# Two graph layers on one core: nodes kept features first, in two halves, between the layers

## The chip, the cores and the metric

The kernel runs on one core of a Trainium2 chip. The core has a matrix engine (TensorE, PE in the profile; its weight loads are PEld), a vector engine (VectorE, DVE), a scalar engine (ScalarE, ACT), GpSimd (POOL) and a sync engine (SyncE, SP) that issues most of the DMA. They run side by side, each in the order of its own instructions, and wait for one another by semaphores. The metric is the device time in microseconds (us); lower is better. One execution was also taken by the hardware profiler; its page and its trace are read here.

## The reference

There are 6250 nodes with 64 features each, and 206250 edges with 16 attributes for the first layer and 64 for the second. Cut to what matters:

```python
h = relu(layernorm(x))
# layer 0: messages along edges, summed at their targets, then a small MLP with batch norm
ea  = edge_attr_16 @ W_edge.T + b_edge
agg = segment_sum(relu(h[src] + ea), dst)
u   = (h + agg) @ W1.T + b1
u   = relu(gamma * (u - mean(u, 0)) * rsqrt(var(u, 0) + 1e-5) + beta)
x   = x + u @ W2.T + b2
h   = relu(layernorm(x))
# layer 1
Y = relu(concat(h[src], edge_attr_64) @ M_W.T + M_b)
Z = segment_sum(Y, dst)
x = x + relu(concat(h, Z) @ U_W.T + U_b)
```

The layer norms have no weights and go over a node's 64 features. The batch norm goes over all nodes, so nothing behind it can start before the whole of layer 0's sums are there.

## The kernel before, in words

The nodes lie in 49 blocks of 128 (NP is 6272), the edges in 101 groups of 16 x 128.

**Sort and layer 0.** Groups 0 to 70 are sorted: POOL scatters their rows by indirect DMA (L786) into a table ordered by block, and 35 blocks are read back, seven chunks each. Such a chunk (class Sorted) turns source and target into one-hot matrices (hot_s L413, hot_d L432) and lets TensorE fetch the sources from the table in SBUF, `tab`, which holds each row as three bf16 parts, and sum the messages (msg L443, L444). Groups 71 to 100 are not sorted (class Direct): POOL gathers their source rows from the table in DRAM (L518, 16 gathers a group, 476 in a layer), and DVE makes the one-hot matrix of the targets (hot_g L565); in layer 0 the message is msg_d (L578), in layer 1 it is made in the gathered tile itself (L574, L575). Work tiles hot_d and msg have two buffers, hot_g and msg_d two more. The gathered tiles have four buffers in layer 0 and five in layer 1. `pace` (L149) ties gathers to TensorE's progress. The end of a block in layer 0 is linear_0 (L809): a product with w1, the bias on ACT into the lower 64 partitions of acc (L816), and batch norm statistics of the block (L820).

**Order.** The sort and layer 0 are written under a manual schedule: PE, DVE and ACT keep the written order there. Everything behind it, the stage between the layers and layer 1, is put in order by a list scheduler (`in_order` L130, L1052), engine by engine, when the kernel is built. SP's loads and stores come in the order of the scheduler too.

**The general case.** `general` (L593) is a loop for edges that found no place. Its count, any_i (L956), is 0 or 49 and is read at run time; here it is 0, so that the loop is entered and left.

**Between the layers (L950 to L1023).** The maximum of the marks gives any_i. The statistics are put together (L980 to L991) to a scale and a shift for each of 64 features, held in 64 partitions. ACT applies them with the relu in place, seven pieces of 64 x 896 (L994). Then a loop over seven chunks of eight blocks: eight products py with a block of acc as the weights (64 x 128) and w2 as the 64 columns moved, so that nodes come to the partitions (L1007); x is loaded (L1009), b2 and py are added (L1010, L1011), and the new x is stored as x1 (L1012); `norm_relu` (L242) makes the layer norm over the free axis; `transposed` (L263) turns the result back to features first in h1t, by eight transposes and two copies on ACT; eight products pt (L1018) make the rows of layer 1's table, mb is added (L1020), the rows are stored to table1 (L1022) and split into the three bf16 parts of tab (L274). The gathers of layer 1 need all of table1.

**Layer 1.** Sorted chunks and Direct halves again, then for each block the output (L1026): two products with uh and uz, the bias, relu and x1 added, a store to out. After it the second call of `general`.

Of the kernel before, what the change touches and what calls it, by code (L numbers as in the profile page):

```python
# [45 lines left out]
P = 128  # L46
D = 64
N = 6250
E = 206250
NB = 49  # L50
NP = P * NB
GT = 16
NG = 101
# [43 lines left out]
def gnn_kernel(  # L97
    ctx: ExitStack,
    tc: tile.TileContext,
    x: bass.AP,  # L100
    src: bass.AP,
    dst: bass.AP,
# [10 lines left out]
    b2: bass.AP,  # L113
    mw_t: bass.AP,
    mb: bass.AP,
    uw_t: bass.AP,
# [154 lines left out]

    tab = const.tile([P, NB, 3, D], BF16, name="tab")

# [267 lines left out]
    class Direct:  # L541
# [20 lines left out]
        def targets(self):  # L562
            n = self.n
            self.hot = self.pool.tile([P, 8, P], F32, name="hot_g", bufs=2)
            nc.vector.tensor_tensor(self.hot[:, :n, :], slot_p[:, None, :].to_broadcast([P, n, P]),  # L565
                                    rel_d[:, self.k:self.k + n, None].to_broadcast([P, n, P]),
                                    op=OP.is_equal)

        def messages(self):
            n = self.n  # L570
            half = slice(8 * self.h, 8 * self.h + n)
            if self.layer == 1:
                self.msg = self.gat[:, half, :]
                nc.vector.tensor_add(self.msg, self.msg, self.ea[:, half, :])  # L574
                nc.scalar.activation(self.msg, self.msg, AF.Relu)  # L575
                return
            self.msg = msg = self.pool.tile([P, 8, D], F32, name="msg_d", bufs=2)[:, :n, :]
            nc.vector.tensor_add(msg, self.pm[:, :n, :], self.gat[:, half, :])  # L578
            nc.scalar.activation(msg, msg, AF.Relu)
            e1 = self.pool.tile([P, 8, D], F32, name="e1", bufs=2)  # L580
            nc.scalar.copy(e1[:, :n, :], self.pe[:, :n, :])
            load(terms[self.g, :, 8 * self.h * D:(8 * self.h + n) * D],
                 e1[:, :n, :].rearrange("p t d -> p (t d)"))
# [6 lines left out]
    marked = const.tile([P, NT], BF16, name="marked")  # L590
    any_i = const.tile([1, 1], I32, name="any_i")

    def general(layer, table, done):  # L593
        blocks = nc.values_load(  # L594
            any_i[0:1, 0:1], min_val=0, max_val=NB,
            skip_runtime_bounds_check_because="it is 0 or NB")
        with tc.tile_pool(name=f"rest{layer}", bufs=1) as rest:
            at_f = rest.tile([P, 1], F32, name="at_f")
            nc.vector.memset(at_f, 0.0)
            delta = rest.tile([P, P], F32, name="delta")  # L600
            with tc.For_i(0, blocks, 1) as b:
                nc.vector.memset(delta, 0.0)
                with tc.For_i(0, NG, 1) as g:
# [39 lines left out]
                    nc.vector.tensor_add(delta, delta, pa[:, 0, :])  # L643
                done(b, delta, rest)
                nc.vector.tensor_scalar(at_f, at_f, float(P), None, op0=OP.add)
# [4 lines left out]
    acc = const.tile([P, NP], F32, name="acc")  # L650
    stats = const.tile([D, NB, 6], F32, name="stats")

    with tc.tile_pool(name="sort", bufs=1) as sort:
# [155 lines left out]
        def linear_0(d):  # L809

            to = acc[:, d * P:(d + 1) * P]

            def product():
                p = bank([D, P], "u_p", "tr")
                mm(p, w1_sb, to, start=True, stop=True)
                nc.scalar.activation(to[:D, :], p, AF.Identity, bias=b1_c)  # L816

            def statistics():
                if d < NB - 1:
                    nc.vector.bn_stats(stats[:, d, :], to[:D, :])  # L820

            return [product, statistics]
# [32 lines left out]
        w1_sb = stacked(w1_t, "w1_sb")  # L855
        b1_c = column(b1, "b1_c")
        for j0, j1 in chunks:
# [43 lines left out]
    for g in range(GS, NG):  # L901
# [5 lines left out]
                                   op0=OP.is_lt, op1=OP.mult)  # L907

    def unsorted(layer, table, steps, per_half, behind, window_of, done):

# [37 lines left out]


    most = ln.tile([P, 1], F32, name="most")  # L950
    nc.vector.tensor_reduce(most, marked, AX.X, OP.max)
    p = bank([P, P], "most_p", "tr")
    nc.tensor.transpose(p, most.to_broadcast([P, P]), ident)
    any_f = ln.tile([1, 1], F32, name="any_f")
    nc.vector.tensor_reduce(any_f, p[0:1, :], AX.X, OP.max)
    nc.vector.tensor_scalar(any_i, any_f, float(NB), None, op0=OP.mult)  # L956

    w2_sb = weight(w2_t, "w2_sb")
    mx_sb = weight(mw_t[0:D, :], "mx_sb")
    uh_sb = weight(uw_t[0:D, :], "uh_sb")  # L960
    uz_sb = stacked(uw_t[D:2 * D, :], "uz_sb")
    b2_b = spread(b2, "b2_b")
    mb_b = spread(mb, "mb_b")
    ub_b = spread(ub, "ub_b")
    gamma_c = column(gamma, "gamma_c")
    beta_c = column(beta, "beta_c")

    def more_0(b, delta, pool):
        p = bank([D, P], "u_p", "tr")
        mm(p, w1_sb, delta, start=True, stop=True)  # L970
        u = pool.tile([D, P], F32, name="u")
        nc.vector.tensor_copy(u, acc[:D, ds(b * P, P)])
        nc.vector.tensor_add(u, u, p)
        nc.vector.tensor_copy(acc[:D, ds(b * P, P)], u)
        s = pool.tile([D, 1, 6], F32, name="s")
        nc.vector.bn_stats(s[:, 0, :], u)
        nc.vector.tensor_copy(stats[:, ds(b, 1), :], s)

    general(0, table0[:, :], more_0)
    nc.vector.bn_stats(stats[:, NB - 1, :], acc[:D, (NB - 1) * P:N])  # L980


    mv = ln.tile([D, 2], F32, name="mv")
    nc.vector.bn_aggr(mv, stats.rearrange("d s k -> d (s k)"))
    bn_scale = ln.tile([D, 1], F32, name="bn_scale")
    bn_shift = ln.tile([D, 1], F32, name="bn_shift")
    nc.scalar.activation(bn_scale, mv[:, 1:2], AF.Sqrt, bias=eps[:D])
    nc.vector.reciprocal(bn_scale, bn_scale)
    nc.vector.tensor_mul(bn_scale, bn_scale, gamma_c)
    nc.vector.tensor_mul(bn_shift, mv[:, 0:1], bn_scale)  # L990
    nc.vector.tensor_sub(bn_shift, beta_c, bn_shift)  # L991
    for a in range(0, NP, NP // 7):
        b = a + NP // 7
        nc.scalar.activation(acc[:D, a:b], acc[:D, a:b], AF.Relu, bias=bn_shift, scale=bn_scale)  # L994


    table1 = dram.tile([NP, D], F32, name="table1")
    table1_rows = table1.rearrange("(j p) d -> p j d", p=P)
    late = ctx.enter_context(tc.tile_pool(name="late", bufs=1))
    h1t = late.tile([D, NP], F32, name="h1t")  # L1000
    x1 = dram.tile([NP, D], F32, name="x1")
    x1_rows = x1.rearrange("(j p) d -> p j d", p=P)
    for j0, j1 in chunks:
        n = j1 - j0
        py = bank([P, 8, D], "py", "gp", 2)
        for j in range(j0, j1):
            mm(py[:, j - j0, :], by_node(acc)[:D, j, :], w2_sb, start=True, stop=True)  # L1007
        xs = ln.tile([P, 8, D], F32, name="xc", bufs=2)[:, :n, :]
        nc.sync.dma_start(xs, x_rows[:, j0:j1, :])  # L1009
        nc.vector.tensor_add(xs, xs, b2_b[:, None, :].to_broadcast([P, n, D]))  # L1010
        nc.vector.tensor_add(xs, xs, py[:, :n, :])  # L1011
        nc.sync.dma_start(x1_rows[:, j0:j1, :], xs)  # L1012
        h = ln.tile([P, 8, D], F32, name="h", bufs=2)
        norm_relu(h, xs)
        transposed(h1t, h, j0, j1)
        pt = bank([P, 8, D], "pt", "gp", 2)
        for j in range(j0, j1):
            mm(pt[:, j - j0, :], by_node(h1t)[:, j, :], mx_sb, start=True, stop=True)  # L1018
        tabf = ln.tile([P, 8, D], F32, name="tabf", bufs=2)
        nc.vector.tensor_add(tabf[:, :n, :], pt[:, :n, :],  # L1020
                             mb_b[:, None, :].to_broadcast([P, n, D]))
        nc.sync.dma_start(table1_rows[:, j0:j1, :], tabf[:, :n, :])  # L1022
        split(tabf, j0, j1)  # L1023


    def output(h_t, z_t, x_b, to, pool):  # L1026
        po = bank([P, D], "po", "pm", 2)
        mm(po, h_t, uh_sb, start=True, stop=False)
        mm(po, z_t, uz_sb, start=False, stop=True)
# [6 lines left out]

    def update(d):
        def product():
            z = acc[:, d * P:(d + 1) * P]
            x_b = late.tile([P, D], F32, name="x_b", bufs=2)  # L1040
            load(x_b, x1_rows[:, d, :])
            output(h1t[:, d * P:(d + 1) * P], z, x_b, out[d * P:(d + 1) * P, :], late)

# [11 lines left out]

    def more_1(b, delta, pool):
        z = pool.tile([P, P], F32, name="z")
        h_t = pool.tile([D, P], F32, name="h_t")
        x_b = pool.tile([P, D], F32, name="x_b")
        nc.vector.tensor_copy(z, acc[:, ds(b * P, P)])  # L1060
        nc.vector.tensor_add(z, z, delta)
        nc.vector.tensor_copy(h_t, h1t[:, ds(b * P, P)])
        nc.sync.dma_start(x_b, x1[ds(b * P, P), :])
        output(h_t, z, x_b, out[ds(b * P, P), :], pool)

# [62 lines left out]
```

## Time and profile before

| what | value |
|---|---|
| nine runs, median | 3138.66 us (3131.61 to 3139.53) |
| profiled execution, own time | 3132.79 us |
| its span | 3131.0 us |
| mean granted tensor clock | 0.819 |
| busy: PE, DVE, ACT, POOL | 2016.7, 1680.4, 641.2, 2066.0 us |
| scatters of the sort on POOL | 37.28 to 1618 us |
| gathers of layer 0 on POOL | 1621.7 to 2216.4 us |
| last statistics of layer 0 | 2222.3 us |
| first gather of layer 1 | 2330.98 us |
| last store to out issued | 3120.17 us |

The page gives each engine's busy time and, for 40 equal slices of the span, its busy tenths. A row of a group of instructions reads: line, engine, operation, what it writes and reads with shapes, how often; then busy time and mean duration of one in ns; then how long the engine had stood idle just before them and what ended that. A row of waits reads: engine, what it wanted to write and its line, who released it, the total in us, how often, the longest. Idle time of an engine that bounds nothing costs nothing, so each stage is read by itself.

### The profile page before, as it was taken

The page shows a single profiled execution, that of the slowest core. Times are in us where ns is not written, and L with a number is a line of the kernel's source. Part 1 is how long each engine was busy: PE and PEld are TensorE (multiplying, and loading weights), DVE is VectorE, ACT ScalarE, POOL GpSimd, SP SyncE. Part 2 cuts the span into 40 slices and gives each one's busy share as a digit, 9 for nine tenths or more (in the row PEclk, how much of TensorE's full clock was granted, in tenths as well). Part 3 has the DMA queues.
Part 4 walks back from the last instruction along what each step waited for, and adds up shares of the span by engine and source line. Part 5 has one row for each costly group of instructions (what it writes and reads, how often), then busy time and mean ns, then how long its engine had stood idle before and what let it go on. Part 6 is the DMA issues. An engine that isn't in the chain of part 4 may idle for free. (4 is left out here: it accounts for less than half of the span.)

```text
span 3131.0 us, 55390 instructions
## 1 busy us (share of the span) xinstructions
PE 2016.7 (64%) x20553; PEld 1589.8 (51%) x20553; DVE 1680.4 (54%) x3532; ACT 641.2 (20%) x1373; POOL 2066.0 (66%) x2098
## 2 busy tenths in 40 slices
PE   2457665575775757576769655555564767776677
PEld 2345554464554545365547444344454656665566
DVE  5756564564765647465625222212343757776576
ACT  2212221121221212122212111111221222222221
POOL 4777777777777777777777777777217456666471
PEclk8688887797887878798889877777657888888798
DMA  9788776888788877788657333333225666776573
GB/s 215 189 233 236 229 205 188 217 238 252 212 229 219 245 197 225 193 239 234 206 175 255 107 84 84 85 87 87 59 59 171 222 199 212 235 232 209 177 249 116
DMA packets 323511, 587.50 MB, mean 188 GB/s; under 512 B 101796, under 2 KB 175908, under 8 KB 314276
## 3 DMA queue, kind: packets, MB, share of 16 engines
q1 hardware_dynamic: 247956, 502.83, 53.3%
q0 software_dynamic: 66816, 79.02, 11.4%
q10 hardware_dynamic: 8464, 2.05, 0.5%
q8 instruction: 163, 2.67, 0.4%
q14 instruction: 112, 0.92, 0.1%
HBM read 382.71 MB, written 200.98 MB: 186 GB/s over the span
## 5 line engine op out<-in xcount | busy, mean ns | idle before, releaser
L786 POOL DMA_INDIRECT place<-to,ix x1136 | 1153.2, 1015 | 458.8 <-issue 241.2
L518 POOL DMA_INDIRECT gat<-table,src_d x952 | 904.7, 950 | 442.1 <-issue 376.4
L141 PE MATMUL pa<-hot_d,msg 128*64 128x128 f32 (+1 forms) x5250 | 716.8, 332 | 116.3 <-ACT msg L444 88.0
L141 PEld LDWEIGHTS pa<-hot_d,msg 128*64 128x64 f32 (+1 forms) x5250 | 551.2, 168 | 179.6 <-ACT msg L444 105.5
L432 DVE TENSOR_TENSOR hot_d<-cbank,dl 128x1024 f32<-128x1024 f32 (+1 forms) x490 | 537.4, 1102 | 124.0 <-PE pa L141 122.4
L141 PEld LDWEIGHTS <-hot_s 128*128 128x128 bf16 x5250 | 202.8, 104 | 304.0 <-DVE hot_s L413 196.2
L141 PE MATMUL gp<-tab,hot_s 128*128 128x64 bf16 x5250 | 217.3, 202 | 150.3 <-DVE hot_s L413 150.3
L141 PE MATMUL gp<-tab,st 128*128 128x64 bf16 x5250 | 224.7, 200 | 52.2 <-DVE msg L443 43.7
L578 DVE TENSOR_TENSOR msg_d<-pm_d,gat 128x512 f32<-128x512 f32 (+1 forms) x60 | 41.2, 687 | 403.6 <-DMA gat<-table,src_d 381.9
L141 PE MATMUL gp<-we,at 128*128 128x512 f32 (+1 forms) x490 | 257.2, 609 | 0.0
L141 PEld LDWEIGHTS <-st 128*128 128x128 bf16 x5250 | 193.3, 103 | 97.9 <-issue 84.3
L141 PE MATMUL pm_d<-we,ea_d 128*128 128x512 f32 x120 | 101.0, 937 | 203.9 <-DVE msg_d L578 203.9
L413 DVE TENSOR_SCALAR hot_s<-st,pcol 128x1024 bf16<-128x1024 bf16 (+1 forms) x245 | 122.5, 500 | 201.8 <-DMA hots<-hot_s 173.3
L444 ACT ACTIVATE msg<-msg 128x512 f32<-128x512 f32 (+1 forms) x245 | 141.8, 584 | 356.8 <-DVE msg L443 346.7
L141 PEld LDWEIGHTS pm<-we,ea 128*128 128x128 f32 x1136 | 179.8, 229 | 28.0 <-DMA ea<-in_ea 17.4
L141 PE MATMUL rk<-half,below 128*128 128x98 bf16 x142 | 19.3, 223 | 270.2 <-DVE half L712 270.2
L141 PE MATMUL pm<-we,ea 128*128 128x128 f32 x1136 | 180.0, 313 | 18.2 <-DMA ea<-in_ea 18.2
L294 ACT COPY at<-at_p 128x128 f32<-128x128 f32 (+1 forms) x245 | 64.6, 264 | 569.5 <-PE at_p L293 564.2
L443 DVE TENSOR_TENSOR msg<-gp,eb 128x512 f32<-128x512 f32 (+1 forms) x245 | 151.5, 627 | 27.8 <-PE gp L141 17.8
L141 PEld LDWEIGHTS <-below 128*128 128x128 bf16 x142 | 14.3, 101 | 284.4 <-issue 263.6
L565 DVE TENSOR_TENSOR hot_g<-cbank,rel_d 128x1024 f32<-128x1024 f32 x120 | 144.7, 1206 | 4.0 <-PE pd L141 3.9
L574 DVE TENSOR_TENSOR gat<-gat,e 128x512 f32<-128x512 f32 (+1 forms) x60 | 40.7, 684 | 184.4 <-DMA gat<-table,src_d 142.1
(139 smaller groups left out, 2357.5 us busy)
## 6 DMA issues: line engine op xcount, KB each, us to landing
eb<-place SPq DMA_DIRECT2D x70, 2050.0 KB
place<-minus SPq DMA_DIRECT2D x35, 2050.0 KB
st<-src_rows SPq DMA_DIRECT2D x210, 256.0 KB
hots<-hot_s SPq DMA_DIRECT2D x210, 256.0 KB
st<-hots SPq DMA_DIRECT2D x210, 256.0 KB
ea<-in_ea SPq DMA_DIRECT2D x71, 512.0 KB
place<-to,ix POOLq DMA_INDIRECT x1136
ea_d<-in_ea SPq DMA_DIRECT2D x30, 512.0 KB
```

What stands on the lines that cost most here:

```text
L141: i = nc.tensor.matmul(*args, **kwargs)
L294: nc.scalar.copy(at[:n * ED, :], p[:n * ED, :])
L413: nc.vector.tensor_scalar(hot_s[:, :n, :], st[:, :n, :], pcol, None, op0=OP.is_equal)
L432: nc.vector.tensor_tensor(self.hot_d[:, :n, :], slot_p[:, None, :].to_broadcast([P, n, P]), self.dl[:, self.a:self.b, :].to_broadcast([P, ...
L443: nc.vector.tensor_add(msg[:, :n, :], gp[:, :n, :], self.eb[:, self.a:self.b, 0:D])
L444: nc.scalar.activation(msg[:, :n, :], msg[:, :n, :], AF.Relu)
L518: i = nc.gpsimd.indirect_dma_start(out=gat[:, t, :], out_offset=None, in_=table, in_offset=bass.IndirectOffsetOnAxis(ap=src_d[:, k:k + 1], ...
L565: nc.vector.tensor_tensor(self.hot[:, :n, :], slot_p[:, None, :].to_broadcast([P, n, P]), rel_d[:, self.k:self.k + n, None].to_broadcast([ ...
L574: nc.vector.tensor_add(self.msg, self.msg, self.ea[:, half, :])
L578: nc.vector.tensor_add(msg, self.pm[:, :n, :], self.gat[:, half, :])
L786: i = nc.gpsimd.indirect_dma_start(out=place[:, :], out_offset=bass.IndirectOffsetOnAxis(ap=ix[:, t:t + 1], axis=0), in_=to[:, t, :], in_o ...
```

## The change

Between the layers the nodes stay features first. They are kept as two halves of 25 blocks, NH = 25: features of blocks 0 to 24 in partitions 0 to 63, those of blocks 25 to 48 in partitions 64 to 127 (the second half has 24 blocks and an empty one). acc, stats, h1t and the batch norm's vectors follow this layout, with weights as two copies on the diagonal of a 128 x 128 matrix or stacked twice.

- W2 is centered beforehand (w2c), and x is loaded features first and centered by a product ahead of layer 0's gathers (xt, less_mean), so that product plus h1t is at once the centered row; its variance is a product with mean_w, and no row is transposed.
- The stage is cut into seven pieces of 512 columns (the last of 128); each goes through nine steps (class Nodes), and a manual schedule runs steps of several pieces in turn.
- The new x (x1) is not needed for the table now. `plain` makes it with products of its own when the table is done, with the loads of x and stores of x1.
- any_i and the weights' loads move ahead of layer 0's gathers; the batch norm's two halves are merged by two small products; `general` runs as two loops, one for each half, in both layers.
- hot_g and msg_d are gone: Direct halves take their tiles from hot_d and msg.

The diff, cut to its core:

```diff
-    tab = const.tile([P, NB, 3, D], BF16, name="tab")
+    tab = const.tile([P, 2 * NH, 3, D], BF16, name="tab")
...
-            self.hot = self.pool.tile([P, 8, P], F32, name="hot_g", bufs=2)
+            self.hot = work.tile([P, 8, P], F32, name="hot_d")
...
-            self.msg = msg = self.pool.tile([P, 8, D], F32, name="msg_d", bufs=2)[:, :n, :]
+            self.msg = msg = work.tile([P, 8, D], F32, name="msg")[:, :n, :]
...
+        for k in range(2):
+            general_half(layer, table, done, k, blocks[k])
...
-                nc.scalar.activation(to[:D, :], p, AF.Identity, bias=b1_c)
+                nc.scalar.activation(acc[half, at], p[half, :], AF.Identity, bias=b1_c[half])
...
+    for half in HALF:
+        nc.vector.memset(mean_w[half, half], 1.0 / D)
+        nc.vector.tensor_scalar(w2c[half, half], w2_2[half], w2m[half], None, op0=OP.subtract)
+        nc.vector.tensor_copy(w2p[half, half], w2_2[half])
+        nc.vector.tensor_copy(mxp[half, half], mx_2[half])
+    nc.vector.tensor_sub(less_mean, ident, mean_w)
...
+    for c in cols:
+        w = c.stop - c.start
+        xs = ln.tile([P, 8, D], F32, name="xc", bufs=2).rearrange("p a d -> p (a d)")[:, :w]
+        nc.sync.dma_start(xs, xt[:, c])
+        p = bank([P, 4 * P], "xt_p", "tr")
+        mm(p[:, :w], less_mean, xs, start=True, stop=True)
+        nc.scalar.activation(h1t[:, c], p[:, :w], AF.Identity, bias=b2m)
...
+    for k, n in enumerate((NH, NB - NH)):
+        nc.vector.bn_aggr(mv[HALF[k]], stats[HALF[k], :n, :].rearrange("d s k -> d (s k)"))
+    bn = bank([P, 2], "bn", "tr")
+    mm(bn[:, 0:1], both, mv[:, 0:1], start=True, stop=True)
+    away = ln.tile([P, 1], F32, name="away")
+    nc.vector.tensor_sub(away, mv[:, 0:1], bn[:, 0:1])
+    nc.vector.scalar_tensor_tensor(mv[:, 1:2], away, away, mv[:, 1:2], op0=OP.mult, op1=OP.add)
+    nc.vector.tensor_sub(mv[:, 0:1], mv[:, 0:1], away)
+    bn = bank([P, 2], "bn", "tr")
+    mm(bn[:, 1:2], both, mv[:, 1:2], start=True, stop=True)
...
+    class Nodes:
...
+        def relu(self):
+            t = acc[:, self.cols]
+            nc.scalar.activation(t, t, AF.Relu, bias=bn_shift, scale=bn_scale)
+        def linear(self):
+            self.y = bank([P, 4 * P], "y", "gp", 2)[:, :self.w]
+            mm(self.y, w2c, acc[:, self.cols], start=True, stop=True)
+        def centered(self):
+            self.cen = mid.tile([P, 4 * P], F32, name="cen", bufs=2)[:, :self.w]
+            nc.vector.tensor_add(self.cen, self.y, h1t[:, self.cols])
+            self.sq = mid.tile([P, 4 * P], F32, name="sq", bufs=2)[:, :self.w]
+            nc.scalar.activation(self.sq, self.cen, AF.Square)
+        def variance(self):
+            self.v = bank([P, 4 * P], "v", "pm", 2)[:, :self.w]
+            mm(self.v, mean_w, self.sq, start=True, stop=True)
+            self.sd = mid.tile([P, 4 * P], F32, name="sd", bufs=2)[:, :self.w]
+            nc.scalar.activation(self.sd, self.v, AF.Sqrt, bias=eps)
+        def norm(self):
+            nc.vector.reciprocal(self.sd, self.sd)
+            nc.vector.scalar_tensor_tensor(h1t[:, self.cols], self.cen, 0.0, self.sd,
+                                           op0=OP.max, op1=OP.mult)
+        def product(self):
+            self.pt = bank([P, 4, 2, D], "pt", ("pa", "rk")[self.c % 2])[:, :self.n]
+            for j in range(self.j0, self.j1):
+                mm(self.pt[:, j - self.j0, :, :].rearrange("p h d -> p (h d)"),
+                   h1t[:, j * P:(j + 1) * P], mxp, start=True, stop=True)
+        def table(self):
...
+            nc.vector.tensor_add(self.tabf, self.pt,
+                                 mb_b[:, None, None, :].to_broadcast([P, n, 2, D]))
+            for k, to in enumerate(by_half(table1_rows, self.j0, self.j1)):
+                if to.shape[1]:
+                    nc.sync.dma_start(to, self.tabf[:, :to.shape[1], k, :])
+            self.part = [tab_h[:, self.j0:self.j1, :, k, :] for k in range(3)]
+            nc.scalar.copy(self.part[0], self.tabf)
+        def second(self):
+            nc.vector.tensor_sub(self.tabf, self.tabf, self.part[0])
+            nc.scalar.copy(self.part[1], self.tabf)
+        def third(self):
+            nc.vector.tensor_sub(self.part[2], self.tabf, self.part[1])
+        def plain(self):
...
+            p = bank([P, 4, 2, D], "px", "gp", 2)[:, :n]
+            for j in range(self.j0, self.j1):
+                mm(p[:, j - self.j0, :, :].rearrange("p h d -> p (h d)"),
+                   acc[:, j * P:(j + 1) * P], w2p, start=True, stop=True)
...
+                    nc.vector.tensor_add(part, part, b2_b[:, None, :].to_broadcast([P, w, D]))
+                    nc.vector.tensor_add(part, part, p[:, :w, k, :])
+                    nc.sync.dma_start(to, part)
...
+        step = ((-1, Nodes.relu), (0, Nodes.linear), (2, Nodes.product), (3, Nodes.second),
+                (0, Nodes.centered), (1, Nodes.variance), (2, Nodes.table), (3, Nodes.third),
+                (1, Nodes.norm))
+        with tc.manual_schedule(engines=ordered):
+            for k in range(-1, len(nodes) + 3):
+                for far, stage in step:
+                    if 0 <= k - far < len(nodes):
+                        stage(nodes[k - far])
+    for n in nodes:
+        n.plain()
```

## The prediction

> **What bounds the kernel now.** The profiled execution took 3132.79 us with a span of 3131.0; the median of the nine runs, 3138.66, is 5.9 above it. I make the sum against 3132.8 and add 5.9 at the end. The page's slices come first: POOL (the gathers and scatters) falls to 1 in slice 29, and the tensor clock is half there.
>
> ```profile
> POOL 4777777777777777777777777777217456666471
> PEclk8688887797887878798889877777657888888798
> ```
>
> The trace puts layer 0's last statistics at 2222.3 us and layer 1's first gather at 2330.98. POOL's waits between 2222 and 2335 (engine, line, releaser; total, times, longest) say what holds it, and the busy times by stretch (PE, PEld, DVE, ACT, POOL, clock, DMA share, GB/s) that no engine is full:
>
> ```profile
> POOL acc L1035 <- PE py L141: 107.4, 1, 107.4
> POOL gat L518 <- DMA table<-tabf: 5.4, 1, 5.4
> 2222.00:2331.00 109.00, 60.80 (x316) 53.13 (x318) 43.91 (x85) 29.52 (x50) 1.72 (x2) 0.51 0.21 52
> 2331.00:2456.00 125.00, 70.27 (x1188) 60.19 (x1188) 62.84 (x92) 25.33 (x46) 76.10 (x81) 0.78 0.55 171
> 2456.00:3060.00 604.00, 436.04 (x7753) 377.40 (x7750) 413.79 (x608) 146.30 (x268) 367.29 (x384) 0.87 0.67 218
> ```
>
> So the 108.7 us from 2222.3 to 2330.98 are a serial chain on the path: the gathers need the whole table. The groups of 2231 to 2331 show its links, above all DVE waiting for PE and PE for DVE:
>
> ```profile
> L141 PE MATMUL pt<-mx_sb,h1t 64*128 64x64 f32 x98 | 22.7, 421 | 0.3 <-ACT h1t L269 0.3
> L141 PE MATMUL py<-w_sb,acc 64*128 64x64 f32 x98 | 22.4, 418 | 9.2 <-ACT acc L994 9.2
> L268 PE MATMUL ht_p<-ident,h 128*64 128x128 f32 x49 | 13.0, 417 | 38.2 <-DVE h L256 34.2 <-ACT h1t L269 4.0
> L1020 DVE TENSOR_TENSOR tabf<-pt,mb_b 128x512 f32<-128x512 f32 (+1 forms) x7 | 4.4, 625 | 33.3 <-PE pt L141 33.3
> L1011 DVE TENSOR_TENSOR xc<-xc,py 128x512 f32<-128x512 f32 (+1 forms) x7 | 4.3, 618 | 18.5 <-PE py L141 18.5
> L255 DVE RECIPROCAL rstd<-var 128x8 f32<-128x8 f32 (+1 forms) x7 | 1.3, 193 | 0.7 <-ACT var L253 0.7
> L246 DVE TENSOR_SCALAR mean<-mean 128x8 f32<-128x8 f32 (+1 forms) x7 | 1.2, 168 | 0.2
> ```
>
> On the timeline L1020 starts at 2247.16, 2262.34, 2277.51, 2292.70, 2308.17 and 2323.35: 15.18 us a chunk of 8 blocks. One chunk is py 3.67, add 0.69, mean 0.69 and 0.17, center 0.69, Square 0.63, sum 0.69, Sqrt 0.30, reciprocal 0.20, norm 0.69, two transposes 1.03 and 1.06 with copies of 0.58, pt 3.67, the rest hand-overs.
>
> **The change part by part.**
>
> *Batch norm, +6.* Now L956 ends at 2223.2, DVE then shows 3.03 us of "issue" (the general loop, which runs no turn), and the shift is ready at 2230.72. After, there is a second loop: +3.0, and 0.8 for its memset, load and turn. Merging the halves adds two tiny matmuls and three DVE operations (0.15 each, L989) with hand-overs: 2 to 3. The any_i chain (2222.39 to 2223.2) goes ahead of layer 0's gathers: -0.8. Shift ready at about 2236.5. If the two loops overlap on the other engines it is +3, if each engine pays for the registers again +9.
>
> *The middle stage itself.* A piece is 4 blocks of both halves (128 rows by 512 columns); six full pieces and one of 128 columns. Per piece PE has linear and variance, one 128x512 f32 matmul each, and a product of four 128x128. Rows: the same 128x512 shape takes two records of 0.51 each at full clock (1.02) and up to 1.06 each for pm_d (2.1); four 128x128 products are 1.05 (pm) to 1.92 (pe_d). So 3.1 a piece at full clock and 6.0 at half. DVE: center, table add, two splits, reciprocal, norm, each 0.69 by the 128x512 rows: 4.1, with gaps 4.4. ACT: relu, Square, Sqrt, two copies, near 0.6 each: 3.0. The loop that closes from one round to the next is product, variance, Sqrt, reciprocal, norm: 1.05+1.02+0.58+0.69+0.69+0.4 = 4.4 at full clock and 6.4 at half. The stage has 0.51 now and would be denser; I take a round at 5.5, between these ends.
>
> The only unknown row is the 128x512 reciprocal. Low end 0.69, as every 128x512 f32 DVE row. High end by the slope of the small shape: 196 ns for 128x8 and 164 for 128x1 is 4.6 ns an element, so 2.5. But L246, a plain multiply, has the same slope (181 and 150 ns), and a plain 128x480 tensor_scalar takes 0.39, so slopes of small shapes mean overhead: I take 0.69 and keep 2.5, which makes a round 8.2 at half clock.
>
> [...]
>
> From 2236.5: relu to the first norm 9.4 (relu 0.6, linear 2, center 0.69, Square 0.63, variance 2, Sqrt 0.6, reciprocal and norm 1.4, hand-overs 1.5); five rounds to the last full product 27.5; the small piece 2.5; 4 for products and adds of plain() that the scheduler lays ahead of the last store, and for the x rows that share SP's queue; last add 1; landing 2.9 (store issued 2328.11, gather 2330.98). First gather at 2236.5+47.3 = 2283.8 against 2330.98: **-47**. Bounds: rounds of 4.4 give -52; 6.4 give -43; with the slow reciprocal -34; all seven plain() products ahead of the last store (1.9 each) another +9, so -25.
>
> [...]
>
> *What plain() moves.* py and its adds leave the chain (counted above). They go on as seven groups of px (1.9), four DVE adds (0.42 each) and stores, beside layer 1's first groups, whose 80 gathers run unbroken anyway for 100 us at 1.245 each from five buffers; PE is busy 70 and DVE 63 of the 125 us there. Seven times 1.9 and 1.7 fit in. Cost 0; if that cover were gone, 13.
>
> *Layer 1.* The code is the same but for the shared tiles; yet nothing holds its order except the scheduler, and that order is changed. What is late here, from 2331 to 3131:
>
> ```profile
> POOL gat L518 <- issue: 268.9, 445, 24.8
> DVE gat L574 <- DMA gat<-table,src_d: 142.1, 24, 12.5
> PE pa L141 <- ACT msg L444: 88.0, 54, 11.0
> DVE hot_d L432 <- PE pa L141: 15.9, 23, 2.2
> ```
>
> No engine is full (PE 559, DVE 526, POOL 455 of 800): gathers stop when all five buffers are held (24.8 us at 2455.93, then 8 to 14 in most groups), and DVE, held at the add L574 for a gather that has not landed, holds back the Sorted messages behind it. How long a group takes goes with where its second half's add stands in DVE's order, counted in Sorted messages past the group's even share of eight: 6 gives 31 to 34 us, 7 gives 28 to 33, 9 and more 20 to 23. This order is fixed when the kernel is built. After the change the place is 8 in eleven groups (no row; 26 between its neighbours), 7 in three, 9 and more in ten: 583 us where the stretch 2456 to 3060 had 604, so -21. The first 103 us stay bound by the gathers: 25 Sorted messages stand ahead of the tenth half's add in both. Sharing hot_d and msg in two buffers instead of two each lets DVE run less far ahead of PE; the wait of this kind is 15.9 us (hot_d), and I add +6, a third of it. Layer 1: **-15**, bounds -76 (every group at its row's low end) and +30 (place gains nothing, shared tiles wait twice as long as hot_d now).
>
> *Layer 0, start and end.* xt, twice() and the diagonal weights come about 1548 us, on SP, ACT, PE and DVE. POOL works off scatters until 1618 without a gap and then gathers at 1.245 without one until 2216; that hides them: 0, and 10 if POOL ran dry. At the start ACT's queue loses about ten weight loads, and SP's gets five small ones: 0, +-2. At the end the last block's output stands behind the first general loop and a second follows: **+4.5** (3 to 6).
>
> Sum: -47-15+4.5 = -57.5; 3075.3 in the profiled execution, **3081** as a median.
>
> **The rivals.** 0.2% (6.3 us) is about what a measurement can tell from no change.
> - *Forecast*, middle and part of layer 1: 3066 to 3095. 0.44.
> - *Only the middle*: layer 1's stalls are set by buffers and latency, not by the place of an add. For: "issue" on POOL recurs in nearly every group. Against: the split by place is clean. -43+4.5, and shared tiles +5 to +20: 3105 (3096 to 3122). 0.20.
> - *Middle at half clock or slow reciprocal*: rounds of 8.2, layer 1 at -5: -34-5+4.5, 3104 (3096 to 3115). For: 0.51 now. Against: L246. 0.12.
> - *Layer 1 much better*: place as good as its best rows, -40: 3056 (3040 to 3066). 0.12.
> - *The pieces do not overlap*: seven serial pieces of some 10 us are 63+9 and later: 3120. Against: DVE, PE and ACT are held to the written order. 0.04.
> - *Slower than before*: two shared buffers tie every Sorted hot_d to a waiting Direct half. The 60 halves of layer 1 each hold a hot tile until their gathers land; if the next Sorted hot then waits, it decides from 62.5/60 = 1.04 us a half on (the middle's and the order's gain, less the end). At 1.4 us: 3160. For: waits of 8 to 12 us on gathers in 24 halves. Against: DVE, in order, is already held at L574 then. 0.08.
>
> Faster: 0.44+0.20+0.12+0.12 and most of 0.04, less tails: 0.89; same 0.03; slower 0.08. The range reaches from inside the better rival to past the serial pieces: 3044 to 3124.
>
> **What would show it.** Right: first gather of layer 1 near 2284; reciprocal 0.69; rounds of 5 to 6; POOL's stalls smaller, group periods near 26; the last store 4 us further from the end of layer 1's last sums. Wrong: reciprocal over 2 us, a first gather after 2300, DVE hot_d waiting for PE above 40 us in layer 1, or POOL pausing between 1618 and 2216.

## The result, and the profile after

The changed kernel takes **3179.29 us** (median of 10 runs, 3170.33 to 3187.01) against 3139.25 for the kernel before (31 runs): a ratio of **1.0127, interval 1.0113 to 1.0141**. It is 40 us slower, where 58 us faster was forecast. Its profiled execution has a span of 3181.1 us.

Both traces can be cut at the same points, all on POOL: the starts of the first and last scatter of the sort, of the first and last gather of layer 0 and of the first and last gather of layer 1, and the end.

| stretch (us) | before | after | difference | forecast |
|---|---|---|---|---|
| scatters of the sort | 1580.8 | 1591.5 | +10.7 | 0 |
| gathers of layer 0 | 593.8 | 606.2 | +12.4 | 0 |
| last gather of layer 0 to first of layer 1 | 115.5 | 82.2 | -33.3 | -47 |
| gathers of layer 1 | 743.0 | 802.6 | +59.6 | -15 |
| from there to the end | 57.0 | 59.8 | +2.8 | +4.5 |

The first row is no effect of the change: over the profiles of this study, apart from those of e9 to e11 below, the scatters, whose code no edit touched, took between 1568.8 and 1598.7 us, in variants of both kernels. The other four rows add up to +41.5; the medians differ by 40.0.

The slices of the page of the changed kernel: POOL's dip is one slice wide now, the 29th counted from one, where it was two, the 29th and 30th (the prediction counts slices from nought), but behind it POOL is at 4 to 6, mostly 5, where it was at 4 to 7 before with four slices of 6 in a row.

```profile
POOL 4777777677777777777766777777164555455551
PEclk7678887898988878798859987877768888888898
```

Busy times by stretch in the changed kernel (as before: PE, PEld, DVE, ACT, POOL, clock, DMA share, GB/s): first the stage between the layers, then the steady part of layer 1.

```profile
2242.40:2318.60 76.20, 40.29 (x135) 26.70 (x136) 51.76 (x70) 21.12 (x37) 1.70 (x1) 0.71 0.21 47
...
2450.00:3107.00 657.00, 453.31 (x7768) 391.02 (x7764) 416.04 (x608) 147.29 (x269) 365.89 (x384) 0.84 0.63 201
```

Now DVE is the busiest engine of the stage, 51.8 of 76.2 us, where PE was. In layer 1 the work of each engine is what it was (DVE 416.0 us here, 413.8 in the 604 us before; POOL 365.9 and 367.3): 24 groups simply take 657 us instead of 604.

**The stage.** The groups of DVE from 2242 to 2319 in the changed kernel:

```profile
L1117 DVE RECIPROCAL sd<-sd 128x512 f32<-128x512 f32 (+1 forms) x7 | 21.1, 3009 | 7.2 <-ACT sd L1114 7.2
L1130 DVE TENSOR_TENSOR tabf<-pt,mb_b 128x512 f32<-128x512 f32 (+1 forms) x7 | 4.4, 632 | 5.1 <-PE pt L144 5.1
L1118 DVE SCALAR_TENSOR_TENSOR h1t<-cen,sd 128x512 f32<-128x512 f32 (+1 forms) x7 | 4.4, 629 | 0.1
```

The reciprocal stands at 21.1 us where every other operation of that shape stands at 4.4. One takes 3.35 us for 128x512 and 0.95 for 128x128: between the two, 6.3 ns for each further element of a partition. One round on the timeline:

```profile
2270.51 3.35 DVE L1117 RECIPROCAL sd<-sd 128x512 f32<-128x512 f32 x1 [1.74 <-ACT sd L1114]
2273.89 0.69 DVE L1118 SCALAR_TENSOR_TENSOR h1t<-cen,sd 128x512 f32<-128x512 f32 x1
...
2274.64 2.08 PE L144 MATMUL pt<-mxp,h1t 128*128 128x128 f32 x8 [3.34 <-DVE h1t L1118]
...
2276.51 1.68 PE L144 MATMUL v<-sq,mean_w 128*128 128x512 f32 x2
...
2278.95 3.35 DVE L1117 RECIPROCAL sd<-sd 128x512 f32<-128x512 f32 x1 [0.91 <-ACT sd L1114]
```

8.44 us from reciprocal to reciprocal: it, the norm, the table product, the variance behind it on PE, the Sqrt, and the next.

**Layer 1.** There are five gather buffers, so a group of gathers needs the buffer of the group five before. Of the 25 groups that have to wait for one, 17 started 0.8 us after the sums of the group five before had ended in the kernel before, and 21 do in the changed one (the expectation of e1 says 20, and four before; the trace shows five). A group came over 5 us late for it 12 times before and 20 times after. One such case in the changed kernel, with POOL, DVE and PE:

```profile
2742.40 0.94 POOL L521 DMA_INDIRECT gat<-table,src_d  x1 [0.30 <-issue]
2745.42 0.69 DVE L577 TENSOR_TENSOR gat<-gat,e 128x512 f32<-128x512 f32 x1 [9.13 <-DMA gat<-table,src_d]
...
2748.58 1.22 DVE L568 TENSOR_TENSOR hot_d<-cbank,rel_d 128x1024 f32<-128x1024 f32 x1
...
2751.59 1.39 PE L144 MATMUL pd<-hot_d,gat 128*64 128x128 f32 x16
...
2753.75 0.94 POOL L521 DMA_INDIRECT gat<-table,src_d  x1 [10.41 <-issue]
```

The last gather of a group is issued at 2742.40. DVE has idled 9.13 us for it and adds at 2745.42. Only behind that add stands the one-hot (2748.58) of the half four groups older, whose sums (2751.59, ended at 2752.98) free the buffer for the next group. So POOL idles 10.4 us. "issue" on POOL is here the wait for a buffer, which the profile does not name.

### The profile page after: what moved, and what is told of

The parts are those of the page before. It is cut to its first block, busy times and chain, and to the rows that moved or that the text cites. A ratio compares the mean times of both kernels' runs of the same rounds, so it can differ in the third digit from the quotient of the medians.

```text
span 3181.1 us, 55523 instructions
## 1 busy us (share of the span) xinstructions
PE 2015.3 (63%) x20456; PEld 1572.3 (49%) x20456; DVE 1701.8 (53%) x3550; ACT 640.0 (20%) x1367; POOL 2067.8 (65%) x2098
## 5 line engine op out<-in xcount | busy, mean ns | idle before, releaser
L435 DVE TENSOR_TENSOR hot_d<-cbank,dl 128x1024 f32<-128x1024 f32 (+1 forms) x490 | 538.5, 1103 | 168.6 <-PE pa L144 153.3
L144 PEld LDWEIGHTS <-st 128*128 128x128 bf16 x5250 | 199.9, 105 | 108.9 <-issue 79.2
L581 DVE TENSOR_TENSOR msg<-pm_d,gat 128x512 f32<-128x512 f32 (+1 forms) x60 | 41.1, 686 | 331.5 <-DMA gat<-table,src_d 331.3
L568 DVE TENSOR_TENSOR hot_d<-cbank,rel_d 128x1024 f32<-128x1024 f32 x120 | 145.1, 1209 | 36.4 <-PE pa L144 21.8
```

The costliest lines, as they stand in the source:

```text
L144: i = nc.tensor.matmul(*args, **kwargs)
L435: nc.vector.tensor_tensor(self.hot_d[:, :n, :], slot_p[:, None, :].to_broadcast([P, n, P]), self.dl[:, self.a:self.b, :].to_broadcast([P, ...
```

## The experiments

Each run is compared with runs of the kernel before on the same chip. The stretches are cut as in the table above, each from one profiled execution. e7 and e8 ran once, so only their stretches are read.

| run | layer 0 gathers | between | layer 1 gathers | to the end | median, ratio to before |
|---|---|---|---|---|---|
| e1_own_tiles | 598.0 | 82.8 | 746.7 | 56.3 | 3121.68, 0.9952 (0.9930 to 0.9974) |
| e2_before_shared | 595.2 | 116.0 | 793.4 | 59.4 | 3190.80, 1.0156 (1.0114 to 1.0197) |
| e3_after_adds_held | 601.7 | 82.3 | 628.1 | 45.5 | 2994.00, 0.9557 (0.9510 to 0.9603) |
| e4_copy_for_reciprocal | 603.5 | 59.4 | 800.1 | 60.3 | 3156.55, 1.0064 (1.0042 to 1.0086) |
| e5_before_adds_held | 594.1 | 115.8 | 607.5 | 48.2 | 2986.80, 0.9533 (0.9504 to 0.9563) |
| e6_held_setup_spread | 595.9 | 82.4 | 629.8 | 46.5 | 2973.90, 0.9486 (0.9456 to 0.9515) |
| e7_variance_first | 606.6 | 74.1 | 807.5 | 59.8 | 3170.85, one run |
| e8_own_hot_only | 607.2 | 82.4 | 743.7 | 57.2 | 3108.99, one run |
| e12_after_best_again | 593.7 | 74.0 | 600.1 | 32.2 | 2924.27, 0.9361 (0.9332 to 0.9389) |
| e13_before_best_again | 594.7 | 115.9 | 600.9 | 28.4 | 2956.22, 0.9463 (0.9437 to 0.9489) |

**e1: own tiles again in the changed kernel.**

```diff
-            self.hot = work.tile([P, 8, P], F32, name="hot_d")
+            self.hot = self.pool.tile([P, 8, P], F32, name="hot_g", bufs=2)
...
-            self.msg = msg = work.tile([P, 8, D], F32, name="msg")[:, :n, :]
+            self.msg = msg = self.pool.tile([P, 8, D], F32, name="msg_d", bufs=2)[:, :n, :]
```

> The changed kernel, but Direct halves have their own hot_g and msg_d tiles again, two buffers each. In the changed kernel's profile layer 1's gathers take 802.6 us (2318.6 to 3121.3) where they took 743.0 before, and 20 of 25 later groups start 0.8 us after the sums of the group four before. Theory (the shared tiles cost it): layer 1's gathers back to 743 +- 10, DVE's order of layer 1 as before the change, kernel near 3179-60 = 3119, faster than both. Rival (plain(), the late loads and stores of x1, or the second loop cost it): layer 1's gathers stay near 800 and the kernel near 3179.

Measured: layer 1's gathers 746.7, the kernel 3121.68. The theory holds: plain(), the second loop and x1 do not cost layer 1 its 60 us. Without this one edit the change would have been half a per cent faster.

**e2: the shared tiles alone in the kernel before** (the same lines the other way round).

> The kernel before, with only this part of the change: Direct halves take their tiles from hot_d and msg. Theory (shared tiles alone cost layer 1 its 60 us): layer 1's gathers 803 +- 10 instead of 743, the kernel near 3139+60 = 3199, slower than both. Rival (the stage between the layers or what follows from it costs it): within 10 us of 3139.

Measured: 793.4 and 3190.80, so +50 in layer 1 and +53 in all. The instructions of layer 1 stand on DVE as in the changed kernel: in 11 of 25 groups the second one-hot of the group four before stands behind both adds of a group, in 11 more between them, and in e1 it is 11 and 3, as before the change. So the shared tiles make the scheduler draw the bad order, in either kernel. Why its list comes out so was not looked into.

**e8: hot_g alone as a tile of its own** (the first two lines of e1).

> The changed kernel with hot_g alone as a tile of its own, msg still shared. Theory (the shared one-hot tile draws the order): DVE's order in layer 1 is that of the kernel before, layer 1's gathers 747 +- 5. Rival (msg, which in layer 1 no Direct half uses, or both): above 780.

Measured: 743.7, and DVE's order is that of e1 (11 and 3). It is the one-hot tile.

**e3: the order written.** Does the order cost the time, or the waits for a free tile?

```diff
+                if len(hots_1) >= 7:
+                    tc.add_manual_dep(i.ins, hots_1[-7].name, ORDER, reason="frees a buffer first")
```

Here i is the add of a gathered half in layer 1, hots_1 the one-hots of the Direct halves so far, and ORDER a dependency without a semaphore.

> The changed kernel with its shared tiles, and one rule of order more: in layer 1 the add into a gathered half stands behind the one-hot of the Direct half seven before on DVE (an order on one engine, no semaphore). So the sums that free a gather buffer stand ahead of the add that waits for the newest gather. Theory (the order on DVE, which the shared tile makes the scheduler draw, is the cause; the tiles themselves cost little): nearly all of POOL's stalls of 6 to 11 us a group go, groups take 20 to 22 us, layer 1's gathers fall to 640-700, the kernel to 3030-3080. Rival (sharing costs by waits for a free tile, whatever the order): layer 1's gathers stay above 780 and DVE waits for PE at hot_d more than the 36 us now.

Measured: layer 1's gathers 628.1, the kernel 2994.00, below both ends of what was expected. The tiles are still shared. Waits in layer 1's gathers (engine, line, releaser; total, times, longest), first of the changed kernel, then of e3, each cut to DVE's adds and its one-hots (L435 and L436 are those of Sorted chunks, L568 and L571 those of Direct halves):

```profile
DVE gat L577 <- DMA gat<-table,src_d: 154.4, 23, 12.3
DVE gat L577 <- issue: 63.1, 13, 8.7
DVE hot_d L435 <- PE pa L144: 26.6, 24, 2.5
...
DVE hot_d L568 <- PE pa L144: 7.3, 9, 1.6
```

```profile
DVE gat L582 <- DMA gat<-table,src_d: 45.2, 7, 11.3
...
DVE hot_d L436 <- PE pa L145: 18.8, 22, 2.9
DVE gat L582 <- issue: 11.2, 4, 5.4
DVE hot_d L571 <- PE pa L145: 8.3, 13, 1.2
```

DVE's wait at the add falls from 217.5 to 56.4 us; its wait for a free one-hot tile hardly moves, from 33.9 to 27.1. The rival falls.

**e5: the same rule in the kernel before.**

> The kernel before, unchanged but for the order rule of the run with the adds held: in layer 1 each add into a gathered half stands behind the one-hot of the Direct half seven before. Theory (order of layer 1 alone, nothing of the change): layer 1's gathers fall from 743 to 628 +- 10 as in the changed kernel with that rule, the kernel from 3139 to 3020 +- 15, and the change is worth 25 +- 10 us once both have the rule (its stage between the layers is 33 us shorter, layer 0's gathers some 8 to 12 longer). Rival (the rule helps because of something in the changed kernel): layer 1's gathers stay above 700.

Measured: 607.5 and 2986.80: further down than expected, and 20 us shorter in layer 1 than e3. So the rule does not need the change, and in e3 something of the change costs layer 1 20 us; 17.5 of them are one stall, the longest wait of POOL there, after the fifth group (first e3, then e5):

```profile
POOL gat L522 <- issue: 157.4, 438, 23.6
```

```profile
POOL gat L519 <- issue: 139.2, 436, 6.1
```

The 25 us that the change was to be worth with the rule in both did not come: the ratios of e3 and e5, 0.9557 and 0.9533, have intervals that overlap. The stretch behind the gathers is shorter with the rule too, 48.2 instead of 57.0 here and 45.5 instead of 59.8 in e3; why was not looked into.

**e4: the price of the reciprocal.**

```diff
-            nc.vector.reciprocal(self.sd, self.sd)
+            nc.vector.tensor_copy(self.sd, self.sd)
```

> The changed kernel with the wide reciprocal of the standard deviation replaced by a copy of it (the layer norm's division is left out; values are wrong downstream, their number and shape the same). The reciprocal took 3.35 us per 128x512, a round of the stage between the layers 8.5. Theory (it lies in the loop product, variance, Sqrt, reciprocal, norm that closes from round to round): a round falls by about 2.7 to 5.8, the stage by 16-19, the kernel to about 3161. Rival (the rounds are set by the tensor engine at half clock, 6.0 us a round, and by the x rows on SP's queue): a round stays above 7 and the gain is under 8 us.

Measured: the stage 59.4 instead of 82.2, rounds of 4.0 to 4.9 (reciprocals, now copies of 0.43, at 2260.44, 2264.43, 2268.94, 2273.53, 2278.40 and 2282.71). The stage between last and first gather, first of the changed kernel, then of e4:

```profile
2236.40:2318.60 82.20, 43.88 (x153) 29.10 (x152) 53.05 (x74) 22.16 (x40) 2.64 (x2) 0.73 0.21 49
```

```profile
2235.10:2294.50 59.40, 32.89 (x152) 21.47 (x151) 35.35 (x74) 21.70 (x40) 2.64 (x2) 0.85 0.29 68
```

That is 22.8 us less, more than the 16 to 19 expected and more than the seven reciprocals save by themselves (21.1 less some 2.8 for the copies, 18.3). The clock in this stage was 0.85 instead of 0.73, and the variance product of a full piece took 1.02 us in all but the first round, where it had taken 1.60 to 1.92. The rival falls.

**e7: the variance product ahead of the table product.**

```diff
-        step = ((-1, Nodes.relu), (0, Nodes.linear), (2, Nodes.product), (3, Nodes.second),
-                (0, Nodes.centered), (1, Nodes.variance), (2, Nodes.table), (3, Nodes.third),
+        step = ((-1, Nodes.relu), (0, Nodes.linear), (1, Nodes.variance), (2, Nodes.product),
+                (3, Nodes.second), (0, Nodes.centered), (2, Nodes.table), (3, Nodes.third),
```

> The changed kernel with one step moved in a round of the stage between the layers: the variance product of the piece behind stands ahead of the table product, not after it. In the changed kernel a round takes 8.4: table product 2.07, variance 1.8, Sqrt 0.69, reciprocal 3.35, norm 0.69 one after the other. Theory (that loop sets the round): it opens, and DVE's own work (3.35 and five times 0.69, 6.8 with nothing between) becomes the bound, rounds of 7 to 7.3, the stage 7 to 9 us shorter than 82.2. Rival (DVE is the bound already or PE's half clock is): rounds stay above 8.

Measured: the stage 74.1; reciprocals at 2253.07, 2259.01, 2266.46, 2273.05, 2280.56 and 2287.30, 6.8 on the average (5.9 to 7.5), and DVE has no idle time ahead of any reciprocal but the first. The loop was the bound, and DVE's own work is the next. The clock in the stage was 0.76.

**e6: the preparation spread over layer 0's groups,** on top of e3.

```diff
                 turn_slot()
+                if layer == 0 and g >= GS + 4:
+                    next(extra, None)
```

extra is a generator of the block with the weights, the diagonals and xt, with a yield behind the loads, behind the matrices and behind each piece of xt.

> The changed kernel with the adds held, and its preparation ahead of layer 0's gathers (weights, diagonal matrices, x features first) put in eleven portions into the groups of layer 0's gathers, from the fifth group on. In the changed kernel DVE's first write of it waits 54.8 us for the last scatter, because its tiles lie where the sort's were, and POOL's gathers pause 12.5 us behind that. Theory (that wait costs layer 0): no wait of over 10 us on that write, POOL pauses under 2 us in layer 0's gathers, which take 594 +- 3 instead of 598 to 606; the kernel 8 +- 8 below the 2994 of the run with the adds held. Rival (the work itself costs it): POOL pauses in the same sum, spread over more groups.

What it takes away, in the waits of DVE of the changed kernel from 1560 to 1760:

```profile
DVE mean_w L962 <- DMA place<-to,ix: 54.8, 1, 54.8
DVE hot_d L435 <- PE pa L144: 51.7, 18, 22.8
```

Measured: the wait is gone; layer 0's gathers 595.9, POOL's pauses in them, beyond the usual 0.3 us between gathers, 1.3 us (none in the kernel before, 12.0 in the changed one, 7.5 in e3); the kernel 2973.90, 20 us below e3 where 0 to 16 were expected. The ratios of e3 and e6 (0.9557 and 0.9486) have intervals that overlap, so the 6 us of layer 0's gathers are what is shown. DVE's first write into the new tiles waited for the last scatter, and DVE ran on only behind it, so the Sorted chunks stood still for 54.8 us. That it is the memory which the write waits for is read from the kernel (the write is a memset and reads nothing); e6 shows that the wait goes when the write comes later. The work itself is hidden, as forecast; its first write was not. The wait alone does not make the 12.4 us of layer 0: with own tiles, in e1, it is 53.5 us long and layer 0's gathers take 598.0, 4 more than before, while with msg shared and hot_g its own, in e8, they take 607.2. So the shared msg tile seems to have a part in it, which no run takes apart.

**e9, e10, e11: all edits together,** and one rule of order more against the stall at the start of layer 1:

```diff
+                if len(sorted_1) >= 17:
+                    tc.add_manual_dep(i.ins, sorted_1[-17].name, ORDER, reason="not ahead of its gather")
```

> The changed kernel with what the runs pointed to: adds held, preparation spread over layer 0's groups, variance product first, and one rule more, that each add into a gathered half also stands behind the Sorted message 16 ahead of the last one written before it (about as many as fit while its gather flies). In the held run the first add stood ahead of all Sorted messages and ahead of plain()'s last adds: DVE idled 10 us for the first gather, and POOL stood 23.6 us for a buffer after the fifth group. Theory (plain() and the early adds take the cover of the first groups): that stall falls under 8 us, layer 1's gathers take 600-610 instead of 630, the stage 74; the kernel 2974-8-22 = 2944 +- 12. Rival (the loads and stores of x1 on SP hold up layer 1's start): the stall stays near 24 and the kernel above 2960.

> The kernel before with both rules of order of layer 1 and nothing else: the partner of the run above. Theory: its first groups have no stall to lose (5.7 us), so 2987 -+ 6. The difference of the two is then what the change's stage is worth when nothing behind it is spoiled: 115.5-74 = 41 us, less the second loop's 3, so 38 +- 10. Rival (layer 1 gives the stage's gain back whatever the order): under 20.

> The run before the last with hot_g and msg_d as own tiles again. Theory (with the order written, sharing the tiles costs little): within 8 us of its partner, DVE's waits for PE at the one-hot tiles a few us less. Rival (the shared tile costs by its waits): faster by over 10 us.

In these three runs everything took a quarter longer, the kernel before beside them too (3916.84 us), with waits that the profile gives to no engine of the core (424.3 us of DVE's waits for hot_d in e9), so these three are compared with one another alone. What made them slow stays open. Measured: 3893.39, 3932.16 and 3895.60; between the layers 97.4, 136.4 and 97.8, layer 1's gathers 1077.2, 1081.5 and 1080.1. The times by themselves are inconclusive; the change is worth 39 us here, and own tiles nothing.

**e12, e13: the first two again.**

> The same kernel as the changed one with all four edits, on another chip than the call in which the kernel before took 3917 us. Theory: 2944 +- 12, the stall after the fifth group under 8 us, layer 1's gathers 600-610. Rival (x1's loads and stores on SP hold up layer 1's start): stall near 24, above 2960.

> The same kernel as the one before with both rules of order. Theory: 2987 -+ 6, and 38 +- 10 above its partner, as in the slow call (39). Rival: less than 20 above it.

These two ran on chip 10, as e9 to e11 did, so that another chip made the difference is not shown. Measured: 2924.27 and 2956.22, both below their ranges; layer 1's gathers 600.1 and 600.9, with no pause of a microsecond in either. The second rule was worth something in the kernel before as well: its ratio falls from 0.9533 (e5) to 0.9463, with 6.6 us less in layer 1's gathers and 19.8 less behind them, which was not forecast. Page slices of POOL of e12, then the stretches of e12 (stage, layer 1), then those of e13:

```profile
POOL 4777777777677777777777777777772477777774
```

```profile
2214.70:2288.70 74.00, 43.42 (x152) 28.06 (x151) 52.79 (x75) 22.48 (x40) 2.65 (x3) 0.71 0.24 55
2288.70:2888.80 600.10, 509.89 (x9625) 436.02 (x9624) 506.78 (x747) 182.26 (x331) 455.32 (x476) 0.97 0.81 269
```

```profile
2202.70:2318.60 115.90, 66.22 (x337) 56.88 (x337) 45.53 (x91) 30.71 (x54) 2.61 (x2) 0.53 0.21 53
2318.60:2919.50 600.90, 507.96 (x9612) 436.94 (x9613) 507.39 (x743) 182.37 (x333) 456.08 (x476) 0.97 0.80 266
```

POOL is at 7 through all of layer 1: the 476 gathers take 600 us, and at the 1.249 from one to the next that most of them take they would need 593. With both kernels there, the change is worth 32 us, within the 38 +- 10 expected: the profiles show 41.9 in the stage less 3.8 at the end, and scatters that took 12.2 us longer in e12, which is no effect of the change. e12 beats both given kernels: 6.4% under the one before.

## Why the prediction was wrong

The sum was -47-15+4.5 = -57.5; the terms measured are -33.3, +59.6, +2.8 and +12.4 in layer 0.

**Layer 1, -15: wrong in sign, and this decided.** The step that failed is "How long a group takes goes with where its second half's add stands in DVE's order, counted in Sorted messages". That place went along with the times in one trace; it is not what POOL waits for. In the changed kernel the places are those forecast, and the times are not: ten of the eleven groups with 8 took 27.0 to 31.5 us, where 26 was taken, and six of the ten with 9 and more took 26.0 to 27.6, where 20 to 23 was taken (one group before had shown it already, 26.2 us with place 11). POOL waits for a buffer, so what counts is whether the one-hot, and with it the sums, of the group four before stand ahead of the adds that wait for the newest gathers: those sums free the buffer of the next group. Groups with that one-hot ahead of both adds took 20.0 to 20.4 us in the changed kernel, those with it behind both 27.0 to 31.5 (those with it between them lie on both sides, 20.4 to 31.3). Read this way the order in which the scheduler lays the instructions, which was known, gives the direction: one-hots behind an add in 14 of 25 groups before, in 22 after. e3 and e5 show the mechanism by taking it away, in both kernels.

**The shared tiles, +6.** They were priced by the wait for a free one-hot tile (15.9 us before). That wait is 33.9 us in the changed kernel, 18 more and below the 40 that were named as a sign of being wrong; it does not make the 59.6. Their effect was to make the scheduler write another order, which is worth +50 (e2) to +56 (the changed kernel against e1) in layer 1's gathers, +53 to +58 in the whole time.

**The rival "slower than before"** was given 0.08. It named the right edit and a price near the one that came (59.6 us in 60 halves, 1.0 us a half, where it decides from 1.04; its 62.5 should be 63.5 by the prediction's own terms, 47+21-4.5), by the wrong mechanism: it is not that "the next Sorted hot then waits" for a tile. That the time came out on its side is luck.

**The stage, -47: right in kind, short by 14.** "I take 0.69" for the reciprocal failed, and so did the high end of 2.5: it takes 3.35. With 3.35 in place of 0.69 the round of 5.5 becomes 8.2, and 8.4 was measured; e7 shows that the loop named is the one that bounds the round. The rival "Middle at half clock or slow reciprocal" had this stage right, -34. The slope of the small shape was the better witness than I allowed: 4.6 ns an element from 128x1 to 128x8, 6.3 from 128x128 to 128x512. That L246 had the same slope proved nothing about the reciprocal: for a plain operation there was a wide row (0.39 us for 128x480) that spoke against its slope, for the reciprocal there was none. Of the 22.8 us that e4 gained the reciprocal itself makes 18.3; the clock was higher there too (0.85 instead of 0.73). Of the rest of this term the batch norm cost +3.7 (8.4 us from the last statistics to the shift before, 12.1 after) where +6 was taken; from the shift to the first gather it is 63.9 instead of 47.3, five rounds of 8.4 instead of 5.5 being 14.5 of it.

**The clock.** 0.71 in the stage (0.73 from gather to gather), so neither the half nor the full that bounded the rounds; with the reciprocal gone 0.85. PE's busy share does not tell these clocks apart: PE was busy 56% of the stage before at 0.51 (8.55 of the 9 us from 2242 to 2251, at 0.50), 53% of it after at 0.73 between the gathers, and 55% in e4 at 0.85; layer 1 of e12, busy 85%, had 0.97. What raised the clock of the stage is not shown.

**Layer 0, 0: wrong.** "POOL works off scatters until 1618 without a gap ...; that hides them: 0, and 10 if POOL ran dry". I counted the operations, and they are hidden; I did not ask where their tiles lie. The first write waited 54.8 us for the last scatter, and POOL paused 12.0 us (e6, on top of e3, takes the wait away and all but 1.3 us of the pauses). Nor are the scatters without a gap in the kernel before: 44 pauses of over a microsecond, the longest 4.7.

**plain(), 0 or 13 if its cover were gone: right, as long as the first groups wait anyway.** Layer 1 with the old order costs 3.7 us more than before (e1). Once the groups run (e3 against e5) 20 us show, and they go when the first adds no longer stand ahead of it (e12, which has the other edits too).

**The end, +4.5:** +2.8. **The start:** first scatter at 35.07 instead of 37.28, within the +-2 forecast but for a fifth of a microsecond; over the other profiles it lies between 34.55 and 37.81, in variants of both kernels.

## What to carry to other kernels

Where a scheduler draws the order, a change of buffers can be a change of order: compare, engine by engine, whether what frees a buffer stands ahead of what waits for the transfer into the next one, and if it does not, write that order down; here that was worth 143 us in the kernel before (2986.80 against 3129.63), over four times the 32 us of the change itself. A row for a small shape does not price a wide one (the reciprocal took 0.20 us for 128x8 and 3.35 for 128x512): an operation that has no wide row in the trace is measured alone before a stage is built around it. A new tile in reused memory may have to wait for the last user of that memory (54.8 us here), so ask of each first write what lay there.

## What the runs showed of the hardware

- A reciprocal on DVE took 3.35 us for 128x512 in f32 and 0.95 for 128x128, 6.3 ns for each further element of a partition; a copy of 128x512 took 0.43 us (e4), the norm of that shape (maximum and product) 0.69.
- The gathers are the floor of layer 1: 476 at 1.249 us, 593 us, met within 8 us when nothing holds POOL (600.1 us in e12), with PE at 510 and DVE at 507 us busy of 600 and a clock of 0.97.
- Apart from e9 to e11 the scatters took 1568.8 to 1598.7 us in the same code, so 30 us of a profile's span can come from them alone.
